# Encoder's end of a two-layer graph network: inverse denominators by transfers, and two node blocks multiplied inside the last attention block

## The chip, the core and the metric

The kernel runs on one core of a Trainium2 chip. The metric is the device time of one execution in microseconds (us). A core has five engines that work side by side, each with its own instruction queue: TensorE (PE in the profile, with PEld for its weight loads), VectorE (DVE), ScalarE (ACT), GpSimd (POOL) and SyncE (SP). Transfers (DMAs) are issued by SP, ACT or POOL and run on 16 shared DMA engines. Matmul results go to PSUM banks of 128 partitions by 512 float32 values, everything else lives in SBUF or in DRAM.

## The reference

Two graph layers on 4096 nodes with 512 features, with one dense 4096 x 4096 mask. The part that matters here is the end of the first layer's encoder and the start of its MLP block (`adj` serves as both patterns, so the two attentions are the same):

```python
Xw = jnp.einsum('hnd,hde->hne', Xh, W)                 # 4 heads of 128 features
sig = jax.nn.sigmoid(f1[:, :, None] + f2[:, None, :])
local_att = _masked_softmax(local_pattern[None] * sig, lmask)
Xa = jnp.einsum('hij,hjd->hid', att, Xw)
Xc = Xa.transpose(1, 0, 2).reshape(n, F)
Xn = _batchnorm(Xc, enc_bn_gamma, enc_bn_beta)         # over the nodes, per feature
emb = _mlp_block(Xn, enc_mlp_W, enc_mlp_b, enc_mlp_bn_gamma, enc_mlp_bn_beta)
# _mlp_block: h = elu(x @ Wm.T + bm) + x, then batchnorm(h)
```

So every output of the attention has to be divided by its softmax denominator, the mean and variance of each feature over all nodes have to be known, and only then can the MLP's product with the normalised features be finished. After it come the decoder (the same attention weights again), its MLP block, and a second graph attention layer, called GAT below.

## The kernel before

All features are kept transposed: a head is a tile of 128 partitions (features) by 4096 nodes, in the tiles R[0] to R[4]. `attention` (L224) runs over 8 *blocks* n, a pair of head and half of the target nodes (2048 each), and in a block over 32 *steps* j of 128 source nodes. In one step ScalarE makes the weight tile e (128 x 2048) with a tanh and an exponential (L571, L572), VectorE multiplies it by the mask (L573), and TensorE multiplies it into four PSUM banks, `po` (L470; the fourth bank joins at step 2, L467). A float32 matmul leaves two records in the profile.

The softmax denominators are sums of e over the steps. Most tiles are summed by VectorE into `acc` (L500, in the last block's last steps L504), some by GpSimd's accumulating transfers into `acc2` (L490), and a few go directly through a matmul with ones (L268). Two last matmul groups with ones turn acc and acc2 into the bank `den`. In blocks 0 to 6 the inverse denominators are made during the next block: a copy of den through DRAM, inverted there in a narrow form (`dcol`, L284 and L285), and sent to all partitions by transfers on GpSimd's queue (L288, L293). Then `scaled` (L686) multiplies each output quarter and `statistics` (L689) takes its mean and variance.

The last block has no next block. Its code begins at L531: the last tile's products (L533, held back so that den comes first), the inverses in one wide form (L546 and L547), the copy of the four outputs out of PSUM (`out_enc`, L683), and for each quarter a matmul with a broadcast column of the identity (L561), which puts the row of inverses on all partitions of a PSUM bank. `scaled` reads that bank. L549 also stores the inverses in DRAM for the decoder.

The MLP block (`mlp_block`, L731) multiplies w (the weights, 4 input blocks by 512 outputs) with the four heads' outputs `xc`. The batchnorm before it is folded in: w is scaled by a_att (`scale_weights`, L696), and its shift becomes part of the bias (`bias_of`, L699, small matmuls with one column each). For heads 0 to 2 this can be done early: `coefs_of_three`, `bias_of_three` and `scale_three` (L710 to L719) are called in the last attention block at steps 10, 12 and 20, through the argument `extras` of L727. After the block, for output block 0, the products of heads 0 to 2 are made for the first 7 of the 8 node blocks (21 matmuls, `product` called at L748), then `last_head` (L776) makes coefficients, bias and weights for head 3, and the 7 sums are completed with its products (L754). There are 7 banks named `ps` (`bank()`) and one named `den` (`bank1()`). The order on each engine is set by a scheduler from the order of the code, with a few explicit ties (`issue_after`, `pinned`).

At the very end of the kernel, GAT's last block already uses another way (L550 to L558): the inverses go to DRAM and come back by four transfers on SyncE's queue into the four parts of acc, and `finish_last` reads these.

Of the kernel before, what the change touches and what calls it, by code (L numbers as in the profile page):

```python
# [39 lines left out]
N, F, H, D, P = 4096, 512, 4, 128, 128  # L40
IB = 512
NIB = N // IB
NJ = N // P
C = IB // P

TB = 2048
NTB = N // TB
SB = TB // IB
# [42 lines left out]
def kernel(ctx, tc, x, xT, adjT, w0, w0T, v0, wencT, wdecT, vecs, w1, w1T, a1, outT):  # L91
    nc = tc.nc
# [10 lines left out]
    w = big.tile([P, C, F], FP, name="w")  # L103

    def nodes(r, ib):
        return r[:, ib * IB:(ib + 1) * IB]
# [4 lines left out]
    def bank():  # L111
        return psum.tile([P, IB], FP, name="ps")
# [12 lines left out]
    ident = consts.tile([P, P], FP, name="ident")  # L125
# [28 lines left out]
    bias = consts.tile([P, C], FP, name="bias")  # L154
# [6 lines left out]
    rinvs = [[dram.tile([1, TB], FP, name=f"rinvs{h}_{t}") for t in range(NTB)] for h in range(H)]  # L161
# [6 lines left out]
    def everywhere(d, row, lo, n):  # L168

        return bass.AP(tensor=d.tensor, offset=d.offset + row * d.shape[-1] + lo, ap=[[0, P], [1, n]])  # L170
# [53 lines left out]
    def attention(what, keep, pools, weights, values, row_of, out, finish, ebufs, modes=None, invert=None,  # L224
                  kept=None, sums=None, sums2=None, extras={}, row0=None, masks0=(), in_parts0=1,
                  finish_last=None, behind=(), fast=None):
# [23 lines left out]
        spool, made, masks0 = pools, 0, list(masks0)  # L250
        if invert is not None:
            acc = spool.tile([P, TB], FP, name="acc") if sums is None else sums
# [143 lines left out]
        for n, (h, tb) in enumerate(blocks):  # L396
            last = n == len(blocks) - 1
# [11 lines left out]
            ahead, late = [], []  # L409
# [121 lines left out]
            for s, b in enumerate(po):  # L531
                for k, t in late:
                    nc.tensor.matmul(b, block(values[h], k), t[:, s * IB:(s + 1) * IB], start=(k == 0),  # L533
                                     stop=(k == NJ - 1))
            if fast is not None:
                combined(h, tb, m)
            outs = [out(spool, h, tb, s, po[s]) for s in range(SB)] if finish_last is None else po
            if invert is None:
                for s, o in enumerate(outs):
                    rb = spread(h, tb, s)  # L540
# [4 lines left out]
            inv = spool.tile([P, IB], FP, name="dsb", tag="rb", bufs=3)  # L545
            nc.vector.tensor_scalar(inv, den, invert[0], None, invert[1])  # L546
            nc.vector.reciprocal(inv, inv)  # L547
            if kept is not None:
                nc.gpsimd.dma_start(rinvs[h][tb].rearrange("o (s i) -> (o s) i", i=IB), inv[0:P:32, :])  # L549
            elif finish_last is not None:  # L550

                nc.sync.dma_start(rinvs[h][tb].rearrange("o (s i) -> (o s) i", i=IB), inv[0:P:32, :])
                rbs = [rb for rb, in in_parts(SB, acc)]
                for s, rb in enumerate(rbs):
                    nc.sync.dma_start(rb, everywhere(rinvs[h][tb], 0, s * IB, IB))
                for s, rb in enumerate(rbs):
                    finish_last(h, tb, s, po[s], rb)
                continue  # L558
            for s, o in enumerate(outs):
                rb = bank()  # L560
                nc.tensor.matmul(rb, ident[:, 32 * s:32 * s + 1].to_broadcast([P, P]), inv, start=True, stop=True)  # L561
                for f in finish:
                    f(spool, h, tb, s, o, rb, True)

    def in_parts(n, *tiles):
        for i in range(n):
            yield tuple(t[:, i * TB // n:(i + 1) * TB // n] for t in tiles)
# [10 lines left out]
    with tc.tile_pool(name="keep", bufs=1) as keep:  # L578

        with tc.tile_pool(name="f_small", bufs=1) as small, tc.tile_pool(name="f_work", bufs=2) as work:  # L580
# [5 lines left out]
            for ib in range(NIB):  # L586
# [7 lines left out]
                for c in range(0, C, 1 if ib == 0 else C):  # L594
                    n = 1 if ib == 0 else C
                    load = nc.sync.dma_start(xs[ib][:, c:c + n, :], xin[:, c:c + n, :])
# [10 lines left out]
            for ib in range(NIB):  # L607
# [15 lines left out]
                for c in range(C):  # L623
                    if ib == 0 and c == 1:
# [3 lines left out]
                    made = (nc.gpsimd if by_pool else nc.vector).tensor_scalar(  # L628
                        hn, xs[ib][:, c, :], mv[:, c, 0:1], rstd[:, c:c + 1], ALU.subtract, ALU.mult)
# [12 lines left out]
                if ib == 0:  # L642

                    pw = bank1()
                    with tc.issue_after(last_pe.ins):
                        for h in range(H):
                            nc.tensor.matmul(pw[:, 2 * h:2 * h + 2], w0Ts[:, h, :], v0s[:, h, :],
                                             start=True, stop=True)
# [4 lines left out]
                for c in range(C):  # L653
                    j = ib * C + c
                    for k in range(2):
                        pv = heads_of(bank())
                        for h in range(2):
                            nc.tensor.matmul(pv[:, h, :], hT[:, 2 * k + h, c * P:(c + 1) * P], w0x[:, 2 * k + h, :],  # L658
                                             start=True, stop=True)
# [19 lines left out]
        xc = [R[4], R[0], R[1], R[2]]  # L679
# [36 lines left out]
        def scale_three(load):  # L716
            nc.vector.tensor_add(bias, banks[0][:, 0:C], vec_of("enc_mlp_b"))
            for fb in range(C - 1):
                scale_weights(fb)  # L719

        with tc.tile_pool(name="enc", bufs=1) as spool:

            with tc.issue_after(last_copy.ins), tc.issue_after(masks0[-1][1].ins):
                attention("enc", keep, spool, tanh_weights, R[0:4], lambda h, tb: (rows[tb], h), out_enc,
                          (scaled, statistics), 6, lambda n: (ENC_FIRST, ENC_SECOND, ENC_THIRD, ENC)[min(n, 3)],
                          (TINY, ALU.max), "write", row0=row0, masks0=masks0,
                          extras={(2, 8): encoder_weights, (H * NTB - 1, 10): coefs_of_three,  # L727
                                  (H * NTB - 1, 12): bias_of_three, (H * NTB - 1, 20): scale_three})


        def mlp_block(work, w, bias, src, dst, gamma, beta, scale, between, early=None):  # L731

            def product(z, o, ib, lo, hi):
                for fb in range(lo, hi):
                    last = nc.tensor.matmul(z, w[:, fb, o * P:(o + 1) * P], nodes(src[fb], ib),  # L739
                                            start=(fb == 0), stop=(fb == C - 1))  # L740
                return last

            for o in range(C):
                zs = {}
                if o == 0:
                    for ib in range(NIB - 1):
                        zs[ib] = bank()
                        product(zs[ib], o, ib, 0, C - 1)  # L748
                    if early is not None:
                        early()  # L750
                for ib in range(NIB):
                    if ib in zs:
                        z = zs[ib]
                        product(z, o, ib, C - 1, C)  # L754
                    else:
                        z = bank()
                        last_product = product(z, o, ib, 0, C)
                    ex = work.tile([P, IB], FP, name="ex")
                    re = work.tile([P, IB], FP, name="re")
                    nc.scalar.activation(ex, z, AF.Exp, bias=bias[:, o:o + 1])  # L760
                    nc.scalar.activation(re, z, AF.Relu, bias=bias[:, o:o + 1])
                    nc.vector.scalar_tensor_tensor(ex, ex, 1.0, re, ALU.min, ALU.add)
                    d = nodes(dst[o], ib)
                    if scale is None:
                        nc.vector.tensor_add(d, nodes(src[o], ib), ex)
                    else:
                        nc.vector.scalar_tensor_tensor(d, nodes(src[o], ib), scale[:, o:o + 1], ex, ALU.mult, ALU.add)
                    made = nc.vector.bn_stats(stats[:, o, ib, :], d)
                    between(o, ib, made)
                bn_coefs(stats, gamma, beta, a_mlp, b_mlp, o, o + 1)  # L770
            return last_product

        with tc.tile_pool(name="m_small", bufs=1) as small, tc.tile_pool(name="m_work", bufs=3) as work:
            yc = [R[3]] + [small.tile([P, N], FP, name=f"yc{o}") for o in range(1, C)]

            def last_head():  # L776
                bn_coefs(stats, "enc_bn_gamma", "enc_bn_beta", a_att, b_att, C - 1, C)
                nc.vector.tensor_add(bias, bias_of(bank1(), C - 1, C)[:, 0:C], bias)
                scale_weights(C - 1)


            behind_it = []
            mlp_block(work, w, bias, xc, yc, "enc_mlp_bn_gamma", "enc_mlp_bn_beta", a_att,
                      lambda o, ib, made: behind_it.append(made) if (o, ib) == (1, 0) else None, last_head)


            for h in range(H):
                w2 = work.tile([P, D], FP, name="w2", bufs=2)
                nc.vector.tensor_scalar_mul(w2, w0Ts[:, h, :], a_mlp[:, h:h + 1])
                bb = work.tile([P, P], FP, name="bb", bufs=1)  # L790
                nc.vector.tensor_scalar_mul(bb, ones, b_mlp[:, h:h + 1])
                pc = bank1()
                nc.tensor.matmul(pc[:, 0:D], bb, w0Ts[:, h, :], start=True, stop=True)
                cr = work.tile([P, 1, D], FP, name="cr", bufs=2)
                nc.vector.tensor_copy(cr[:, 0, :], pc[:, 0:D])
                for ib in range(NIB):
                    pv = bank().rearrange("p (c d) -> p c d", d=D)
                    for c in range(C):
                        nc.tensor.matmul(pv[:, c, :], block(yc[h], ib * C + c), w2, start=True, stop=True)  # L799
                    nc.vector.tensor_add(nodes(xc[h], ib).rearrange("p (c d) -> p c d", d=D), pv,  # L800
                                         cr.to_broadcast([P, C, D]))
# [15 lines left out]
        z = w.rearrange("p c f -> p (c f)")[:, 0:4 * PAIRS * HD].rearrange("p (i k c) -> p i k c", i=4, c=HD)  # L817
# [310 lines left out]
```

## Time and profile before

| what | us |
|---|---|
| median of 3 runs | 3199.43 |
| lowest and highest of them | 3197.14, 3202.03 |
| the profiled execution | 3198.86 |
| its span | 3197.1 |
| transition that the change touches: last record of L470 in the encoder to the first product of head 3 | 1025.22 to 1056.22 |

The profile is one execution; times in its views count from the start of its span. A line of a timeline gives start, length, engine, line of the kernel, operation, output and input with their shape, the number of records, and in square brackets the idle time before and what ended it. A line of the windows gives, for each stretch, the busy time and records of each engine in the order PE, PEld, DVE, ACT, POOL, then the granted TensorE clock, the DMA share and GB/s. Line numbers are those of the kernel before; the changed kernel's lie a few lower in this part.

### The profile page before, as it was taken

The numbers are of one execution on the slowest core, as the hardware profiler recorded it, in microseconds if no ns is written. First come the engines' busy times: TensorE is split into PE (matmuls) and PEld (weight loads), VectorE is DVE, ScalarE is ACT, GpSimd is POOL, SyncE is SP. The second block draws the span as 40 slices with busy tenths as digits, with TensorE's granted clock in tenths as the row PEclk, the third lists the DMA queues.
The fourth block names the chain that finished last, engine by engine and source line by source line (L and its number), as shares of the span: only waits on it lengthen the run. The fifth ranks groups of instructions, "written<-read, shape, count | busy, mean of one in ns | idle before, by whom it ended". The sixth has DMA issues, their size and how long they took to land.

```text
span 3197.1 us, 30054 instructions
## 1 busy us (share of the span) xinstructions
PE 3146.9 (98%) x10539; PEld 1371.7 (43%) x10539; DVE 2938.7 (92%) x2222; ACT 2573.7 (81%) x1825; POOL 525.9 (16%) x680
## 2 busy tenths in 40 slices
PE   7999999999999999999999999999999999999998
PEld 6334444444444463333333333458544444444443
DVE  7989999999999678999999999685699999999998
ACT  7999999999998449999999999466755665666663
POOL 3001211211211000010100100026312222222221
PEclk9999999999999999999999999999999999999999
DMA  9998978988987014444445454322579999899996
GB/s 212 198 194 253 267 209 233 271 223 229 267 227 190 7 44 148 155 159 156 160 162 165 141 168 145 97 105 74 149 193 228 219 219 243 217 213 229 236 213 156
DMA packets 214792, 589.25 MB, mean 184 GB/s; under 512 B 25872, under 2 KB 28976, under 8 KB 198640
## 3 DMA queue, kind: packets, MB, share of 16 engines
q0 software_dynamic: 71008, 231.95, 37.9%
q1 hardware_dynamic: 132200, 332.53, 30.1%
q10 hardware_dynamic: 11432, 22.85, 2.0%
q8 instruction: 83, 1.36, 0.2%
q14 instruction: 69, 0.57, 0.1%
HBM read 378.15 MB, written 84.30 MB: 145 GB/s over the span
## 4 chain that ended last, share of the span: by engine, by line
PE 68%; DVE 15%; issue 8%; ACT 5%; DMA 3%; DVEq 0%; ACTq 0%; POOL 0%; POOLq 0%; SPq 0%
PE ps L470 28%; PE ps L332 22%; PE ps L739 7%; DVE e L573 5%; DVE acc L500 4%; PE den L332 3%; PE ps L950 3%; ACT e L571 3%; DMA a<-mask 3%; DVE R L500 2%; ACT e L572 2%; DVE e L1045 2%; PE den L268 1%; PE ps L799 1%; PE ps L658 1%
## 5 line engine op out<-in xcount | busy, mean ns | idle before, releaser
L470 PE MATMUL ps<-e,R 128*128 128x512 f32 x3992 | 1737.9, 595 | 19.2 <-DVE e L573 16.6
L470 PEld LDWEIGHTS ps<-e,R 128*128 128x128 f32 x3992 | 754.6, 190 | 998.8 <-issue 921.6
L573 DVE TENSOR_TENSOR e<-e,a 128x2048 f32<-128x2048 f32 (+1 forms) x470 | 1049.5, 2261 | 80.2 <-ACT e L572 66.9
L571 ACT ACTIVATE e<-rowb,score 128x2048 f32<-128x2048 f32 (+1 forms) x470 | 909.1, 1969 | 20.3 <-PE ps L332 8.9
L572 ACT ACTIVATE e<-e 128x2048 f32<-128x2048 f32 (+1 forms) x470 | 866.9, 1879 | 4.4 <-DVE e L573 0.7
L332 PE MATMUL ps<-e,R 128*64 128x512 f32 x2624 | 746.8, 592 | 1.6 <-DVE e L573 1.5
L1044 ACT ACTIVATE e<-rowb,nq,jcol 128x2048 f32<-128x2048 f32 x224 | 459.6, 2088 | 263.3 <-DMA w<-e 133.1
L1045 DVE SCALAR_TENSOR_TENSOR e<-e,jcol,a 128x2048 f32<-128x2048 f32 (+1 forms) x265 | 592.9, 2271 | 2.8 <-ACT e L1044 2.8
L332 PEld LDWEIGHTS ps<-e,R 128*64 128x64 f32 x2624 | 241.9, 137 | 319.7 <-issue 316.2
L500 DVE TENSOR_TENSOR R<-R,e 128x2048 f32<-128x2048 f32 x128 | 292.5, 2285 | 0.0
L500 DVE TENSOR_TENSOR acc<-acc,e 128x2048 f32<-128x2048 f32 x122 | 278.7, 2284 | 1.0
L490 POOL DMA_DIRECT2D w<-e x178 | 151.9, 865 | 605.8 <-DMA w<-e 293.1
L739 PE MATMUL ps<-R,w 128*128 128x512 f32 x512 | 220.4, 592 | 0.6 <-DVE w L697 0.6
L490 POOL DMA_DIRECT2D acc<-e x142 | 119.1, 893 | 521.3 <-DMA acc<-e 238.4
L739 PEld LDWEIGHTS ps<-R,w 128*128 128x128 f32 x512 | 97.1, 190 | 123.0 <-issue 117.7
L332 PE MATMUL den<-e,R 128*64 128x512 f32 x320 | 149.8, 592 | 0.0
L332 PE MATMUL ps<-e,w 128*64 128x512 f32 x288 | 138.1, 592 | 0.7 <-DVE e L573 0.7
L293 POOL DMA_DIRECT2D rb<-rinvs x60 | 34.5, 578 | 520.7 <-DVE R L687 449.4
L950 PE MATMUL ps<-w1x,hT 128*128 128x260 f32 x512 | 115.5, 384 | 1.4 <-ACT hT L928 1.4
L332 PE MATMUL ps<-t,w 128*64 128x512 f32 x336 | 111.3, 592 | 1.1 <-DVE t L341 1.1
L950 PEld LDWEIGHTS ps<-w1x,hT 128*128 128x128 f32 x512 | 96.5, 190 | 19.9 <-issue 3.4
L332 PE MATMUL ps<-t,R 128*64 128x512 f32 x192 | 90.2, 592 | 0.0
(209 smaller groups left out, 2115.5 us busy)
## 6 DMA issues: line engine op xcount, KB each, us to landing
a<-mask SPq DMA_DIRECT2D x720, 256.0 KB, 4.3
w<-e POOLq DMA_DIRECT2D x178, 512.0 KB, 6.8
acc<-e POOLq DMA_DIRECT2D x142, 512.0 KB, 7.1
e<-ekeep SPq DMA_DIRECT2D x48, 1024.0 KB, 5.1
ekeep<-e SPq DMA_DIRECT2D x36, 1024.0 KB, 7.1
mask<-in_adjT POOLq DMA_DIRECT2D x8, 2048.0 KB, 105.0
rowb<-rows SPq DMA_DIRECT2D x16, 1024.0 KB, 5.5
rb<-rinvs POOLq DMA_DIRECT2D x60, 256.0 KB, 4.7
```

The source lines that it names most:

```text
L293: hop.dma_start(rb, everywhere(rinvs[h][tb], 0, s * IB, IB))
L332: last_half = nc.tensor.matmul(b[g * HD:(g + 1) * HD, :], weight, x, start=start, stop=stop)
L470: last_main = nc.tensor.matmul(b, block(values[h], j), e[:, s * IB:(s + 1) * IB], start=(j == 0), stop=(j == NJ - 1))
L490: nc.gpsimd.dma_start(into_half, e_half, **({"accum_op": ALU.add} if j > moved[0] else {}))
L500: nc.vector.tensor_add(acc, acc, e)
L571: nc.scalar.activation(e, rowb, AF.Tanh, bias=column(score[:, 1], j, h), scale=0.5)
L572: last_act = nc.scalar.activation(e, e, AF.Exp, scale=0.5)
L573: last_dve = nc.vector.tensor_mul(e, e, a)
L739: last = nc.tensor.matmul(z, w[:, fb, o * P:(o + 1) * P], nodes(src[fb], ib), start=(fb == 0), stop=(fb == C - 1))
L950: m = nc.tensor.matmul(banks[k][:, 0:2 * DX], hT[:, fb, c * P:(c + 1) * P], w1x[:, fb, 2 * k:2 * k + 2, :].rearrange("p h x -> p (h x)"), ...
L1044: last_act = nc.scalar.activation(e, rowb, AF.Relu, bias=column(nq, j, h), scale=column(jcol, j, h))
L1045: last_dve = nc.vector.scalar_tensor_tensor(e, e, column(jcol2, j, h), a, ALU.add, ALU.mult)
```

## The change

Three edits, all at the encoder's end:

1. The four broadcast matmuls of L561 go away. The last block of the encoder now does what GAT's last block does: inverses to DRAM, then four transfers of a row to all partitions, into the four parts of acc. For the encoder they are issued on ScalarE's queue. GAT's end stays as it was.
2. Coefficients, bias and scaled weights of heads 0 to 2 are made at steps 1, 4 and 6 of the last block instead of 10, 12 and 20.
3. The products of heads 0 to 2 for node blocks 0 and 1 (output block 0, 6 matmuls) are made inside the last block, called at steps 9 and 12; `mlp_block` is given their banks and makes the remaining 15.

```diff
-            if kept is not None:
-                nc.gpsimd.dma_start(rinvs[h][tb].rearrange("o (s i) -> (o s) i", i=IB), inv[0:P:32, :])
-            elif finish_last is not None:
-
-                nc.sync.dma_start(rinvs[h][tb].rearrange("o (s i) -> (o s) i", i=IB), inv[0:P:32, :])
-                rbs = [rb for rb, in in_parts(SB, acc)]
-                for s, rb in enumerate(rbs):
-                    nc.sync.dma_start(rb, everywhere(rinvs[h][tb], 0, s * IB, IB))
-                for s, rb in enumerate(rbs):
+            queue = nc.scalar if kept is not None else nc.sync
+            queue.dma_start(rinvs[h][tb].rearrange("o (s i) -> (o s) i", i=IB), inv[0:P:32, :])
+            rbs = [rb for rb, in in_parts(SB, acc)]
+            for s, rb in enumerate(rbs):
+                queue.dma_start(rb, everywhere(rinvs[h][tb], 0, s * IB, IB))
+            for s, rb in enumerate(rbs):
+                if finish_last is not None:
                     finish_last(h, tb, s, po[s], rb)
-                continue
-            for s, o in enumerate(outs):
-                rb = bank()
-                nc.tensor.matmul(rb, ident[:, 32 * s:32 * s + 1].to_broadcast([P, P]), inv, start=True, stop=True)
+                    continue
                 for f in finish:
-                    f(spool, h, tb, s, o, rb, True)
+                    f(spool, h, tb, s, outs[s], rb, True)
...
+        def product(src, w, z, o, ib, lo, hi):
+            for fb in range(lo, hi):
+                last = nc.tensor.matmul(z, w[:, fb, o * P:(o + 1) * P], nodes(src[fb], ib),
+                                        start=(fb == 0), stop=(fb == C - 1))
+            return last
+
+        zs_ahead = {}
+
+        def product_ahead(ib):
+            def f(load):
+                zs_ahead[ib] = bank()
+                product(xc, w, zs_ahead[ib], 0, ib, 0, C - 1)
+            return f
...
-                          extras={(2, 8): encoder_weights, (H * NTB - 1, 10): coefs_of_three,
-                                  (H * NTB - 1, 12): bias_of_three, (H * NTB - 1, 20): scale_three})
+                          extras={(2, 8): encoder_weights, (H * NTB - 1, 1): coefs_of_three,
+                                  (H * NTB - 1, 4): bias_of_three, (H * NTB - 1, 6): scale_three,
+                                  (H * NTB - 1, 9): product_ahead(0), (H * NTB - 1, 12): product_ahead(1)})
...
-        def mlp_block(work, w, bias, src, dst, gamma, beta, scale, between, early=None):
-            def product(z, o, ib, lo, hi):
...
+        def mlp_block(work, w, bias, src, dst, gamma, beta, scale, between, early=None, ahead={}):
             for o in range(C):
                 zs = {}
                 if o == 0:
-                    for ib in range(NIB - 1):
+                    zs.update(ahead)
+                    for ib in range(len(zs), NIB - 1):
                         zs[ib] = bank()
-                        product(zs[ib], o, ib, 0, C - 1)
+                        product(src, w, zs[ib], o, ib, 0, C - 1)
                     if early is not None:
                         early()
```

More of the change, by code (lines that the diff above doesn't have):

```diff
@@ L726 @@
                           (TINY, ALU.max), "write", row0=row0, masks0=masks0,
-                          extras={(2, 8): encoder_weights, (H * NTB - 1, 10): coefs_of_three,
-                                  (H * NTB - 1, 12): bias_of_three, (H * NTB - 1, 20): scale_three})
-        def mlp_block(work, w, bias, src, dst, gamma, beta, scale, between, early=None):
-            def product(z, o, ib, lo, hi):
[L738 to L741, printed above, removed]
+                          extras={(2, 8): encoder_weights, (H * NTB - 1, 1): coefs_of_three,
+                                  (H * NTB - 1, 4): bias_of_three, (H * NTB - 1, 6): scale_three,
+                                  (H * NTB - 1, 9): product_ahead(0), (H * NTB - 1, 12): product_ahead(1)})
+        def mlp_block(work, w, bias, src, dst, gamma, beta, scale, between, early=None, ahead={}):
             for o in range(C):
@@ L753, in mlp_block @@
                         z = zs[ib]
-                        product(z, o, ib, C - 1, C)
+                        product(src, w, z, o, ib, C - 1, C)
                     else:
                         z = bank()
-                        last_product = product(z, o, ib, 0, C)
+                        last_product = product(src, w, z, o, ib, 0, C)
                     ex = work.tile([P, IB], FP, name="ex")
@@ L783 @@
             mlp_block(work, w, bias, xc, yc, "enc_mlp_bn_gamma", "enc_mlp_bn_beta", a_att,
-                      lambda o, ib, made: behind_it.append(made) if (o, ib) == (1, 0) else None, last_head)
+                      lambda o, ib, made: behind_it.append(made) if (o, ib) == (1, 0) else None, last_head,
+                      zs_ahead)
             for h in range(H):
```

## Prediction

> **What bounds the kernel now.** I read the page first: which engine is full, and over how much of the span.
>
> ```profile
> span 3197.1 us, 30054 instructions
> PE 3146.9 (98%) x10539; PEld 1371.7 (43%) x10539; DVE 2938.7 (92%) x2222; ACT 2573.7 (81%) x1825; POOL 525.9 (16%) x680
> ```
>
> TensorE is full for 98% of the span, so a change pays only by taking work off TensorE where it is the late engine, or by filling a hole in it. Then I read the timeline of all engines across the end of the encoder, which is all that the change touches:
>
> ```profile
> 1025.22 1.92 PE L268 MATMUL den<-e,ones 128*32 128x512 f32 x16
> ...
> 1028.79 3.70 PE L533 MATMUL ps<-e,R 128*128 128x512 f32 x8
> 1028.93 0.69 DVE L546 TENSOR_SCALAR dsb<-den 128x512 f32<-128x512 f32 x1 [1.70 <-PE den L268]
> ...
> 1029.66 3.35 DVE L547 RECIPROCAL dsb<-dsb 128x512 f32<-128x512 f32 x1
> ...
> 1033.06 3.70 PE L561 MATMUL ps<-dsb,ident 128*128 128x512 f32 x8 [0.57 <-DVE dsb L547]
> ...
> 1036.60 18.19 PE L739 MATMUL ps<-R,w 128*128 128x512 f32 x42
> ...
> 1054.62 0.95 PE L702 MATMUL den<-coefs,w 128*128 128x1 f32 x8
> ...
> 1056.22 19.15 PE L739 MATMUL ps<-R,w 128*128 128x512 f32 x44 [0.65 <-DVE w L697]
> ```
>
> The reader is to see one TensorE chain without a real hole: denominators, last tile (L533), broadcast of the inverses (L561), 21 products that need only heads 0 to 2 (L739; a matmul leaves two records here, 0.429 us apart), bias, then the products of head 3. Is TensorE also late in the eighth block before it? The timelines of TensorE's weight loads and of VectorE say yes but for one place, step 25:
>
> ```profile
> 1004.42 0.30 PEld L470 LDWEIGHTS ps<-e,R 128*128 128x128 f32 x2 [0.92 <-DVE e L573]
> ```
>
> The usual idle time there is 0.24 us, so TensorE waited 0.68 us for that tile. Last, windows of 1 us gave the granted clock (the number after the brackets):
>
> ```profile
> 958.00:959.00 1.00, 1.00 (x3) 0.42 (x3) 1.00 (x2) 1.00 (x1) 0.12 (x1) 0.96 1.08 238
> 959.00:960.00 1.00, 1.00 (x2) 0.33 (x1) 1.00 (x1) 1.00 (x2) 0.73 (x1) 0.50 0.92 160
> 960.00:961.00 1.00, 1.00 (x2) 0.33 (x1) 1.00 (x2) 1.00 (x1) 0.00 (x0) 0.50 1.13 289
> 961.00:962.00 1.00, 1.00 (x3) 0.44 (x2) 1.00 (x1) 1.00 (x2) 0.00 (x0) 0.50 1.05 274
> 962.00:963.00 1.00, 1.00 (x4) 0.44 (x3) 0.86 (x1) 1.00 (x1) 0.78 (x1) 0.83 1.06 309
> ```
>
> Half rate from about 959.0 to 962.4, just behind the 12 one-column bias matmuls (L702, 955.16 to 957.8): some 1.7 us lost. So there is far less slack in this block than the records' count suggests.
>
> **What the Trainium skill says.** "TensorE: Matmul & The Clock Gate", Part 1, What's actually happening: the array runs at half rate after a low-activity window of about 3.4 us, and the window is free-running. The trace agrees: one dip of 3.4 us at 0.50, behind 2.6 us of one-column work. "DMA: Bandwidth & Descriptors", Two DMAs through the same engine are not ordered: a read of what another transfer wrote must wait for that one's semaphore. Here too: at the kernel's end the write issues at 3182.7 and the first read at 3184.5. Same page, Issuing engines are not separate DMA queues: SyncE's and ScalarE's transfers share the 16 engines, so SyncE's route is a fair price for ScalarE's.
>
> **The change part by part.** T is the end of the denominators (1028.86 before).
>
> *Broadcast off TensorE.* L533's last slot ends at 1028.79 + 8 x 0.429 = 1032.22 and L739 starts at 1036.60: 4.38 us leave TensorE (3.43 of L561, 0.95 of waits around it). -4.38.
>
> *Six products moved into the block.* 6 x 2 x 0.429 = 5.14 us leave the chain behind T. -5.14.
>
> *What they cost inside the block.* As built, three products stand between steps 8 and 9, three before step 12. TensorE works without a hole from 911.8 to step 25: it starts step 2 at 918.78 where VectorE's timeline has the tile by 913.5, step 10 at 948.2 against 940.7. So all 5.14 us push it, less the hole at step 25: +5.14 - 0.68 = +4.46, and T is at about 1033.3.
>
> *Coefficients from step 10 to 1, bias from 12 to 4, scaling from 20 to 6.* No instruction is added. On ScalarE two table loads of 1.28 us and a 0.20 us root (938.44 to 941.25) move ahead of step 4's tile; ScalarE is full either way and is where it was from step 12 on. On VectorE the bias sum (0.12) and the scalings (1.18, 981.49 to 982.67) move from behind to ahead of its idle stretch (1.15, 1.77, 0.97, 0.57 and 0.69 us at L573 from 938 to 963). Tiles 4 to 9 come some 2.5 to 4.5 us later, and TensorE has 6 us in hand at each: cost 0. Tile 25 comes 1.3 us earlier (1003.1), while TensorE arrives at 1008.9, so the hole is gone, and VectorE's last sums are done by about 1026, TensorE needing them at 1031.9. The sum for step 4 makes VectorE wait for the bias matmuls (they end near 928.2, VectorE arrives at 926.8): 1.5 us, soaked up by the same idle stretch. The dcol inversion falls 4 us later, and POOL's rinvs and rb transfers behind it too; their rb is wanted at 965.8, was issued at 945.6, and here near 950 with 4.7 us to land (median of rb on POOL's queue). Cover 10 us; were it late, only VectorE's lead of 5 us would go.
>
> *The new route.* The kernel's own end runs it on SyncE's queue, shown by VectorE's timeline:
>
> ```profile
> 3179.35 3.35 DVE L547 RECIPROCAL dsb<-dsb 128x512 f32<-128x512 f32 x1
> 3187.75 0.75 DVE L1064 SCALAR_TENSOR_TENSOR R<-ps,ssum,R 128x512 f32<-128x512 f32 x1 [5.05 <-DMA R<-rinvs]
> 3188.77 0.75 DVE L1064 SCALAR_TENSOR_TENSOR R<-ps,ssum,R 128x512 f32<-128x512 f32 x1 [0.27 <-DMA R<-rinvs]
> ```
>
> 5.05 us from the inverses to the first product, parts about 1 us apart. At the encoder's end no other transfer runs (0.02 MB from 1026 to 1060), and ScalarE has nothing behind the five issues but the root for head 3 and its table load. After: inverses at T + 4.15 (1033.01 - 1028.86), first scaling at T + 9.20, four scalings and four statistics 4.85 (1035.26 to 1040.11), coefficients 1.6 (1040.14 to 1041.72): T + 15.65. TensorE, with 15 products left, loads the first bias weight at 1054.20 - 1028.86 - 4.38 - 5.14 = T + 15.82. Cover: 0.17 us. Bounds: below nothing is excluded, since the 15 products have to run first whatever lands early; if the parts land 1 us late, 0.8 us of stall; I take 0, as the only measured route gives it. All seven banks are now held at T (four outputs, bias, two ahead); the first product behind L533 gets the bias bank, the next needs L683's first copy at T + 4.8 and is due at T + 5.9: 0.
>
> *POOL* loses one issue (0.59 us), on nobody's path. SyncE's order is unchanged, and so is everything behind the encoder.
>
> Sum: -4.38 - 5.14 + 4.46 = -5.06 us. The profiled execution took 3198.86 (its span 3197.1), giving 3193.8; the median shown is 0.57 higher, so 3194.4.
>
> **The rivals.**
>
> A, *the forecast*: the dip comes again behind the moved bias matmuls, 3194.4.
>
> B, *no dip this time*. Before, a missing dip gains nothing, since TensorE would only wait longer at step 25. After, nothing waits there, so 1.6 us more are saved: -6.7, 3192.7. For it: the window is free-running, and the bias matmuls fill only 2.6 of 3.4 us. Against it: the neighbours are as dense as before.
>
> C, *the cover runs out*. With 0.17 us of cover, a route 2 to 3 us longer stalls TensorE as much, and a longer lull could call up another dip: gain 1 to 3, about 3197.4. For it: the thin cover. Against it: the route measured at the kernel's end.
>
> D, *the transfers replace the broadcast as the bound*, slower. In earlier blocks rinvs took 6.9 us (POOL's queue) and rb 7.4 (ScalarE's): 14.3 instead of 5.05, a stall of 9.1, +4.0 us, with a dip +5.7: 3203.4 to 3205.1. It decides from a route of 10.1 us on. Against it: those ran beside full DMA engines, here they are idle.
>
> That the change doesn't do what it says: the built order shows every move, so I give this nothing.
>
> **How the numbers follow.** A 0.50, B 0.25, C 0.14, D 0.06, 0.05 for what I don't see, half of it slower. 0.2% is 6.4 us, about what a measurement of this kernel can tell from no change; the three runs before spread over 4.9 us. With that scatter A passes 6.4 in three of ten, B in six of ten: faster 0.30. Slower by that much: part of D and of the unseen, 0.07. The rest, 0.63, is within. Range: 3191.3 (B with scatter) to 3198.3 (C).
>
> **What would show it.** T near 1033.3; no L561; step 25 without idle time; the idle time of TensorE between the 15 products and L702 under 0.5 us; head 3's first product at about 1051.2 instead of 1056.2; clock 0.50 near 930 (A) or not (B). Wrong if TensorE waits for a tile between steps 2 and 12, or if the first scaling comes later than 6 us behind the inverses.

## The result and the profile after

The kernel after takes 3192.33 us (median of 11 runs, 3190.36 to 3196.14) against 3199.38 us for the kernel before beside it (11 runs, 3196.71 to 3202.03): a ratio of 0.998, interval 0.9973 to 0.9988. In a second series it took 3192.54 us (17 runs) against 3199.12 us (63 runs), ratio 0.9981 (0.9974 to 0.9988). The means differ by 6.4 and 6.2 us in the two series. The profiled execution of after took 3192.33 us, its span is 3190.4 us.

The page of after, its first lines (span; busy time, share and instructions of each engine):

```profile
span 3190.4 us, 30044 instructions
PE 3139.7 (98%) x10531; PEld 1368.4 (43%) x10531; DVE 2938.4 (92%) x2222; ACT 2573.5 (81%) x1825; POOL 522.3 (16%) x679
```

TensorE's busy time fell by 7.2 us and its instructions by 8: four broadcast matmuls, two records each.

The timeline of TensorE in after, from the last encoder block's start to head 3's products:

```profile
908.15 1.93 PE L268 MATMUL den<-e,ones 128*32 128x512 f32 x16
...
925.56 2.73 PE L697 MATMUL ps<-coefs,w 128*128 128x1 f32 x24
...
947.10 2.74 PE L718 MATMUL ps<-R,w 128*128 128x512 f32 x6
...
962.03 2.74 PE L718 MATMUL ps<-R,w 128*128 128x512 f32 x6
964.60 65.40 PE L470 MATMUL ps<-e,R 128*128 128x512 f32 x152
...
1031.67 1.90 PE L268 MATMUL den<-acc,ones 128*32 128x512 f32 x16
1033.50 3.70 PE L533 MATMUL ps<-e,R 128*128 128x512 f32 x8
1037.04 13.04 PE L718 MATMUL ps<-R,w 128*128 128x512 f32 x30
1049.91 0.95 PE L697 MATMUL den<-coefs,w 128*128 128x1 f32 x8
1051.51 23.87 PE L718 MATMUL ps<-R,w 128*128 128x512 f32 x55 [0.65 <-DVE w L692]
```

The broadcast is gone, L718 follows L533 with nothing between, 15 products instead of 21 (30 records instead of 42) stand behind the block, and two groups of three stand inside it. The bias matmuls run at 925.56 instead of 955.16. Head 3's first product starts at 1051.51 (1056.22 before).

VectorE at the same place, the first scaling and what it waited for; then TensorE's weight load of head 3's bias matmuls:

```profile
1034.44 3.35 DVE L547 RECIPROCAL dsb<-dsb 128x512 f32<-128x512 f32 x1
...
1042.80 0.69 DVE L682 TENSOR_TENSOR R<-R,acc 128x512 f32<-128x512 f32 x1 [2.67 <-DMA acc<-rinvs]
...
1049.37 0.16 DVE L186 TENSOR_TENSOR coefs<-vec,coefs 128x1 f32<-128x1 f32 x1
```

```profile
1049.65 1.12 PEld L697 LDWEIGHTS den<-coefs,w 128*128 128x128 f32 x8 [0.41 <-issue]
```

The scaling now waits for the transfer, as it should; the coefficients come at 1049.53 and the load that needs them follows 0.12 us later, with 0.41 us of idle time instead of the usual 0.24. The cover is used up to the last tenth.

Windows of 2 us of after, of TensorE alone:

```profile
926.00:928.00 2.00, 2.00 (x20) 1.00 0.55 205
928.00:930.00 2.00, 2.00 (x7) 0.81 1.00 199
930.00:932.00 2.00, 2.00 (x4) 0.50 1.15 223
932.00:934.00 2.00, 2.00 (x5) 0.84 0.87 216
```

The half-rate stretch is there again, behind the bias matmuls in their new place: (0.19 + 0.50 + 0.16) x 2 = 1.7 us lost.

To compare executions I use D, the time from the first denominators matmul of encoder block 6 (L268, 908.15 here) to head 3's first product. It takes out whatever ran differently before: in the thirteen profiles of this document D starts between 907.40 and 910.91. D is 147.98 us before and 143.36 after: -4.62. The kernel before starts it here; its end, 1056.22, is in the prediction:

```profile
908.24 1.92 PE L268 MATMUL den<-e,ones 128*32 128x512 f32 x16
```

Nothing is lost or won again until the last block of GAT: the first matmuls behind the encoder's MLP (L799 at 1148.39 before, L800 at 1143.67 after) and VectorE's last tile (it ends at 3173.81 before, 3169.07 after) are both 4.7 us earlier. From head 3's first product to that tile, twelve of the thirteen profiles have 2117.56 to 2117.60 us; the exception, e4, is explained below.

Of the other 2 us of the 6.7 between the spans, 1.8 arise at the kernel's very end, the last block of GAT, which the change doesn't touch. TensorE there, before and then after:

```profile
3169.40 1.06 PE L268 MATMUL den<-e,ones 128*32 128x512 f32 x8 [2.33 <-DVE e L1045]
3170.40 1.76 PE L533 MATMUL ps<-e,R 128*128 128x512 f32 x2
3173.87 1.94 PE L268 MATMUL den<-e,ones 128*32 128x512 f32 x8 [1.71 <-DVE e L1045]
3175.57 1.94 PE L268 MATMUL den<-w,ones 128*32 128x512 f32 x8
3177.28 1.19 PE L268 MATMUL den<-R,ones 128*32 128x512 f32 x8
```

```profile
3164.65 1.67 PE L268 MATMUL den<-e,ones 128*32 128x512 f32 x8 [2.32 <-DVE e L1046]
...
3169.12 1.06 PE L268 MATMUL den<-e,ones 128*32 128x512 f32 x8 [0.79 <-DVE e L1046]
3170.00 1.04 PE L268 MATMUL den<-w,ones 128*32 128x512 f32 x8
3170.86 1.04 PE L268 MATMUL den<-R,ones 128*32 128x512 f32 x8
```

The same eight records take 1.94 us in one and 1.04 in the other. TensorE waits for VectorE's tiles here, and in both executions the granted clock falls to 0.50: before, from 3170.8 to 3177.6, under the last three groups, so that the denominators end 4.66 us behind VectorE's last tile; after, from 3165.0 to 3168.4, where the wait for the next tile takes it in, and they end 2.83 us behind it. That is which part of the end the stretch meets in one execution, and says nothing of the change: e6 below, whose encoder is that of the kernel before but for the order of its bias matmuls, ends as after does, and e7, a form of the changed kernel, has a late end (4.3 us).

### The profile page after: what moved, and what is told of

It reads as the page before. It is cut to its first block, busy times and chain, and to the rows that moved or that the text cites. A ratio compares the mean times of both kernels' runs of the same rounds, so it can differ in the third digit from the quotient of the medians.

```text
span 3190.4 us, 30044 instructions
## 1 busy us (share of the span) xinstructions
PE 3139.7 (98%) x10531; PEld 1368.4 (43%) x10531; DVE 2938.4 (92%) x2222; ACT 2573.5 (81%) x1825; POOL 522.3 (16%) x679
## 4 chain that ended last, share of the span: by engine, by line
PE 54%; DVE 21%; issue 12%; ACT 8%; DMA 4%; DVEq 0%; POOL 0%; ACTq 0%; POOLq 0%; SPq 0%
PE ps L332 22%; PE ps L470 14%; PE ps L718 7%; DVE e L1046 6%; DVE R L500 6%; ACT e L566 5%; DVE e L568 4%; PE den L332 3%; PE ps L951 3%; DVE acc L500 3%; ACT e L567 3%; DMA a<-mask 3%; PE den L268 1%; PE ps L800 1%; DMA acc<-e 1%
## 5 line engine op out<-in xcount | busy, mean ns | idle before, releaser
L718 PE MATMUL ps<-R,w 128*128 128x512 f32 x512 | 220.8, 592 | 0.6 <-DVE w L692 0.6
L718 PEld LDWEIGHTS ps<-R,w 128*128 128x128 f32 x512 | 97.1, 190 | 123.0 <-issue 116.7
```

## The experiments

Two theories stood at the start. The first: taking the broadcast off TensorE brings the 4.4 us, and the products moved ahead add only what they fill of the hole at step 25. The rival: the moves bring it, and the route costs more than it saves. Later the question became why the medians differ by more than D. All results first; the ratio is against the kernel before in the same series, and "half rate" is what each one's profile shows between steps 1 and 16 of the last encoder block.

| kernel | median us (runs) | ratio, interval | D us | half rate |
|---|---|---|---|---|
| before | 3199.38 (11) | | 147.98 | yes |
| after | 3192.33 (11) | 0.998 (0.9973 to 0.9988) | 143.36 | yes |
| e1, route alone | 3193.79 (21) | 0.9987 (0.9981 to 0.9994) | 143.73 | no |
| e2, moves alone | 3197.25 (13) | 0.9996 (0.9988 to 1.0004) | 147.69 | yes |
| e3, one block ahead | 3191.54 (14) | 0.9979 (0.9971 to 0.9987) | 141.67 | no |
| e4, three blocks ahead | 3196.56 (13) | 0.9995 (0.9987 to 1.0004) | 144.09 | no |
| a2, after again | 3192.54 (17) | 0.9981 (0.9974 to 0.9988) | 141.67 | no |
| e5, after, bias split | 3192.00 (21) | 0.9981 (0.9975 to 0.9988) | 141.72 | no |
| e7, one ahead, bias split | 3192.28 (19) | 0.9981 (0.9974 to 0.9988) | 141.67 | no |
| e8, as e7, busy end | 3191.40 (17) | 0.9978 (0.9971 to 0.9986) | 141.67 | no |
| e6, before, bias split | 3197.25 (13) | 1.0000 (0.9992 to 1.0008) | 147.98 | no |
| e9, after, busy end | 3192.25 (19) | 0.9983 (0.9976 to 0.9989) | 143.59 | yes |
| e10, before, busy end | 3197.67 (13) | 0.9999 (0.9990 to 1.0007) | 147.99 | yes |

The kernel before took 3198.06 us beside e1 to e4, 3199.12 beside a2 to e8 and 3197.45 beside e6, e9 and e10.

**e1, the route alone.** Coefficients, bias and scaling back at steps 10, 12 and 20, no product ahead, and the 21 products tied behind the last tile, so that none of them can be scheduled into the block:

```diff
-                          extras={(2, 8): encoder_weights, (H * NTB - 1, 1): coefs_of_three,
-                                  (H * NTB - 1, 4): bias_of_three, (H * NTB - 1, 6): scale_three,
-                                  (H * NTB - 1, 9): product_ahead(0), (H * NTB - 1, 12): product_ahead(1)})
+                          extras={(2, 8): encoder_weights, (H * NTB - 1, 10): coefs_of_three,
+                                  (H * NTB - 1, 12): bias_of_three, (H * NTB - 1, 20): scale_three})
...
-                        product(src, w, zs[ib], o, ib, 0, C - 1)
+                        with pinned(tail):
+                            product(src, w, zs[ib], o, ib, 0, C - 1)
```

> Route alone: coefficients, bias and scaling stay at steps 10, 12 and 20, no product is made ahead, all 21 are tied behind the last tile; only the broadcast goes by transfers. D is the time from the first denominator matmul of block 6 to head 3's first product: 147.98 us before, 143.36 after. Theory (the route carries nearly all of the gain, 4.38 us, because the 21 products hide it): D 143.6, time about 3195. Rival (the moved products carry it, and the route alone saves only the 0.95 us of waits): D 147, time about 3198.5.

D is 143.73, 4.25 us under the kernel before, as the first theory has it. The coefficients come at 1044.16, and the weight load that waits for them is due at 1049.10, so 4.9 us of cover stand where after has none. The timeline shows both ends of D, and between them what the moves would still have to give:

```profile
907.40 1.92 PE L270 MATMUL den<-e,ones 128*32 128x512 f32 x16
...
1003.60 20.87 PE L472 MATMUL ps<-e,R 128*128 128x512 f32 x48 [1.80 <-DVE e L570]
...
1051.13 24.30 PE L720 MATMUL ps<-R,w 128*128 128x512 f32 x56 [0.65 <-DVE w L694]
```

The hole at step 25 is open, and wider than in the kernel before, which had a half-rate stretch ahead of it.

**e2, the moves alone.** After, with the broadcast by matmul in place of the route:

```diff
-            queue = nc.scalar if kept is not None else nc.sync
-            queue.dma_start(rinvs[h][tb].rearrange("o (s i) -> (o s) i", i=IB), inv[0:P:32, :])
...
+            for s, o in enumerate(outs):
+                rb = bank()
+                nc.tensor.matmul(rb, ident[:, 32 * s:32 * s + 1].to_broadcast([P, P]), inv, start=True, stop=True)
```

> Moves alone: coefficients at 1, bias at 4, scaling at 6, two node blocks ahead, but the broadcast is again the four matmuls of before. Theory (TensorE is late in the block too, so moving fills only the hole at step 25): D 147.3 with a half-rate window behind the bias, 145.7 without one, time about 3198.5 or 3197. Rival (the moved products carry the gain): D 143.5, time about 3194.5.

D is 147.69, with the half-rate stretch at 930 to 935: the moves alone are worth 0.3 us in such an execution. The rival falls. The median is 0.8 us under the kernel before, an interval that includes no change.

**e3 and e4, one and three node blocks ahead.** e3 drops the product at step 12 (and ties the other 18 behind the last tile), e4 adds one at step 15:

```diff
-                                  (H * NTB - 1, 9): product_ahead(0), (H * NTB - 1, 12): product_ahead(1)})
+                                  (H * NTB - 1, 9): product_ahead(0), (H * NTB - 1, 12): product_ahead(1),
+                                  (H * NTB - 1, 15): product_ahead(2)})
```

> The changed kernel with one node block ahead instead of two, the other 18 products tied behind the last tile. Theory (a moved product costs TensorE the same inside the block; one block of 2.57 us already fills the hole): D 143.4, the same as after, and the cover of the transfers is 2.6 us longer, so TensorE doesn't wait for head 3's coefficients. Rival (each moved block pays 2.57 us): D 145.9.

> The changed kernel with a third node block ahead, at step 15, so that 12 products are left to hide the transfers. Theory (the cover is used up at two, so the denominators come 2.57 us later and nothing is given back): D 145.9, with TensorE idle 2.6 us before the bias matmuls of head 3, time about 2.6 us above after. Rival 1 (there is slack in the block): D 143.4. Rival 2 (each moved block pays): D 140.8.

e3's D is 141.67 without a half-rate stretch:

```profile
908.41 1.92 PE L270 MATMUL den<-e,ones 128*32 128x512 f32 x16
...
1050.08 25.16 PE L720 MATMUL ps<-R,w 128*128 128x512 f32 x58 [0.65 <-DVE w L694]
```

The kernel after without a stretch (a2 below) has 141.67 as well, so the second node block ahead buys nothing; it only takes the cover, 2.5 us here (counted to the weight load; the expectation of e7 counts 2.9 to the matmul behind it), down to none. In e4 the limit shows. TensorE's timeline, then the windows behind it:

```profile
1039.20 10.57 PE L718 MATMUL ps<-R,w 128*128 128x512 f32 x24 [1.19 <-DVE R L678]
...
1050.49 1.02 PE L697 MATMUL den<-coefs,w 128*128 128x1 f32 x8 [0.72 <-DVE coefs L186]
```

```profile
1050.00:1052.00 2.00, 1.02 (x8) 1.00 0.00 0
1052.00:1054.00 2.00, 1.84 (x4) 0.82 0.00 0
1054.00:1056.00 2.00, 2.00 (x4) 0.50 0.00 0
1056.00:1058.00 2.00, 2.00 (x5) 0.83 0.00 0
```

With 12 products left behind the block TensorE waits for a bank and then for the coefficients. The third block costs its 2.57 us inside and saves almost nothing behind (17.79 us from the denominators to head 3's first product, 17.94 in after): D is 2.42 us above e3's. The longer lull is followed by a half-rate stretch of its own, and VectorE's last tile of GAT comes 1.7 us later for it, 2119.27 us behind head 3's first product. Together that is 4.1 of the 4.5 us by which e4's mean gain (1.7) falls short of e3's (6.2) in the same series.

**a2, the kernel after once more**, and **e5**, with its bias matmuls spread out:

```diff
+        def bias_part(o):
+            def f(load):
...
+                for fb in range(C - 1):
+                    nc.tensor.matmul(banks[0][:, o:o + 1], w[:, fb, o * P:(o + 1) * P], b_att[:, fb:fb + 1],
+                                     start=(fb == 0), stop=(fb == C - 2))
...
-                                  (H * NTB - 1, 4): bias_of_three, (H * NTB - 1, 6): scale_three,
+                                  **{(H * NTB - 1, 3 + o): bias_part(o) for o in range(C)}, (H * NTB - 1, 8): scale_three,
```

> The kernel after once more, unedited. D is the stretch from the first denominators matmul of encoder block 6 to head 3's first product behind the last block: 143.36 us in its first profile, with the half-rate clock stretch behind the bias matmuls of step 4 in it. Theory (the half-rate stretch falls or doesn't fall by chance, and there is no slack left in the last block to soak it up): D is either 143.4 with it or 141.7 without it, and nothing between. Rival (the stretch follows the bias matmuls every time): D 143.4 again, half rate near 930.

> The kernel after, with the twelve one-column bias matmuls in four parts of three at steps 3 to 6 and the weights scaled at step 8. Theory (a lull of 2.6 us of one-column matmuls is what lets the clock fall; four lulls of 0.65 us are too short for it): no half-rate stretch in the last block, D 143.36 - 1.65 = 141.7, and the median at or below the kernel after's of the same call, by 0 to 1.7 us, by how often the kernel after has the stretch. Rival (the stretch has another cause than the lull): half rate again between 925 and 940, D 143.4.

The same program, another execution. TensorE's timeline and windows in a2:

```profile
908.00 1.92 PE L268 MATMUL den<-e,ones 128*32 128x512 f32 x16
...
925.41 2.73 PE L697 MATMUL ps<-coefs,w 128*128 128x1 f32 x24
...
1048.07 0.95 PE L697 MATMUL den<-coefs,w 128*128 128x1 f32 x8
1049.67 12.71 PE L718 MATMUL ps<-R,w 128*128 128x512 f32 x29 [0.65 <-DVE w L692]
```

```profile
928.00:930.00 2.00, 2.00 (x7) 1.00 1.02 201
930.00:932.00 2.00, 2.00 (x6) 1.00 1.06 209
```

Full rate throughout, and D = 1049.67 - 908.00 = 141.67, which is 1.69 us less. So the program alone doesn't decide whether the stretch comes, and in after it is paid in full. Among the profiles with the undivided lull it is in before, after, e2, e9 and e10, and not in e1, e3, e4 and a2; among the four with the lull in parts (e5, e6, e7, e8) in none. Five of nine against none of four points to the lull, without settling it. The median of e5 is 0.5 us under a2's, which these runs can't tell from nothing.

**e6, the same split in the kernel before.**

```diff
-                                  (H * NTB - 1, 12): bias_of_three, (H * NTB - 1, 20): scale_three})
+                                  **{(H * NTB - 1, 12 + o): bias_part(o) for o in range(C)}, (H * NTB - 1, 20): scale_three})
```

> The kernel before, with its twelve bias matmuls in four parts of three at steps 12 to 15, one step's products between them. Theory (the kernel before has slack in its last block: TensorE reaches tile 25 before VectorE has made it, so that half rate ahead of it is taken out of the wait): no half rate, the wait at step 25 grows from 0.68 to about 2.3 us, D stays 147.98, the time that of the kernel before within 0.5 us. Rival (half rate costs the kernel before its 1.65 us as well): the wait stays 0.68, D 146.3, the time 1.6 us less where the stretch would have fallen.

D is 147.98 again, to the hundredth, without a half-rate stretch, and the time that of before. TensorE's weight loads at step 25 of e6, to be held against the line shown in the prediction (0.92 us of idle time there):

```profile
1001.54 0.19 PEld L470 LDWEIGHTS ps<-e,R 128*128 128x128 f32 x1 [0.24 <-issue]
1004.34 0.30 PEld L470 LDWEIGHTS ps<-e,R 128*128 128x128 f32 x2 [2.61 <-DVE e L573]
1004.88 0.19 PEld L470 LDWEIGHTS ps<-e,R 128*128 128x128 f32 x1 [0.24 <-issue]
```

What the clock doesn't take, the wait takes: tile 25 sets the time in the kernel before. On this point the two kernels differ: after has no wait there that could take the stretch in.

**e7, e8, e9, e10: a busy end.** e7 is e3 with the bias matmuls split; e8 is e7, e9 after and e10 before, each with two matmuls whose product nobody reads ahead of each of the last two terms of the denominators in GAT's last block (the expectations say decoder; the edit acts only where `finish_last` is set, and that is GAT's):

```diff
                     if held and j + 1 not in by_ones:
-                        with tc.issue_after(last_main.ins):
-                            for t in held:
+                        for t in held:
+                            if finish_last is not None and last and j == NJ - 1:
+                                last_main = stay_busy(last_main, 2)
+                            with tc.issue_after(last_main.ins):
                                 add_to_den(den, t, not begun)
...
```

> One node block multiplied ahead instead of two, and the bias matmuls in four parts. Theory (the second node block ahead buys nothing, since the coefficients of head 3 then come no earlier than TensorE needs them, and the split keeps the clock up): head 3's bias matmuls wait for nothing, cover 2.9 us, no half rate in the last block, D 141.7 as in the one-ahead run; median about 3198.2 - 7 = 3191. Rival (one block ahead leaves 0.86 x 3 us more behind the last block): D 141.7 + 2.57 = 144.2.

> The kernel of one block ahead and split bias, and in the decoder's last attention block two idle matmuls of 512 columns ahead of each of the last two denominators' terms, where TensorE otherwise waits 2.3 us for VectorE's weights. Their product is not used. Theory (the last 1.8 us of the difference between the two kernels came from a half-rate stretch that these waits bring about at the kernel's end, earlier or later by chance): no half rate behind 3160, the denominators end 2.9 us behind VectorE's last addition, and the slow end of the run-to-run spread goes; median 0 to 1.8 us under the same kernel without them. Rival (that stretch is no matter of these waits): half rate near the end as often as before, the same median, or slower by the 0.86 us of the product that now comes behind.

> The kernel after, with the two pairs of unused 512-column matmuls at the decoder's end only. Theory (half rate at the kernel's end, brought about by TensorE's two waits there, costs up to 1.9 us in some runs): no half rate behind 3160, the denominators end 2.9 us behind VectorE's last addition, the median 0.5 to 1.5 us under the kernel after's, some 3191.4. Rival (no matter of these waits): half rate there as before, median as the kernel after's, 0.9981 of before.

> The kernel before, with the two pairs of unused 512-column matmuls at the decoder's end only; its encoder is not touched. Theory (the half rate at the end has nothing to do with the change, and the kernel before pays for it as well): no half rate behind 3160, the denominators end 2.9 us behind VectorE's last addition instead of 4.74, median 0.5 to 1.8 us under the kernel before. In its encoder D is 148.0 whether or not the half-rate stretch falls there: with it the wait at step 25 is 0.7, without it 2.3. Rival: no difference from the kernel before, and D 146.3 without the half-rate stretch.

e7 confirms e3: D 141.67, and head 3's bias matmuls wait for nothing. With the busy end no profile shows half rate between 3160 and 3180 (none of three), and the denominators end 2.8 us behind VectorE's last tile; without it six of ten profiles do, though only before and e7 with a cost at the end. But the medians did not move: 0.9983 for e9 against 0.9981 for a2, 0.9999 for e10, and e8 0.9 us under e7, within the intervals. VectorE's last product in e10 shows a price:

```profile
3191.31 0.75 DVE L1068 SCALAR_TENSOR_TENSOR R<-ps,ssum,R 128x512 f32<-128x512 f32 x1 [0.47 <-PE ps L537]
```

The idle matmuls displace a real product that had run in the wait (32 records of it stand behind the denominators now, 30 before), and the last output waits for TensorE, 0.47 us in e10, 0.40 in e9 and 0.29 in e8. Whether that price alone keeps the median where it was isn't shown. The highest times are lower (3199.18 in e10, 3200.62 for the kernel before beside it; 3194.97 in e9, 3195.89 and 3196.14 in after), but e10's 13 runs stand against 39; the theory's gain in the median did not come. e8 has the lowest median of all, but none of e3, e7 and e8 can be told from the kernel after.

## Why the prediction was right, and where it was off

The forecast's direction and mechanism held: the route alone brings 4.25 us, as e1 shows with the moves taken away, and the moves bring what they fill of the hole. The time forecast, 3194.4, came out 2 us too high; rival B's 3192.7 is nearer. That the measured median lies in the forecast's range is partly luck: the range had room for A and for B, and no step of the forecast had GAT's end, which moved by 1.8 us between the two profiles. By its steps:

- *Broadcast off TensorE, -4.38.* e1 measured -4.25. Right.
- *Six products behind T, -5.14.* From T to head 3's first product the profile has 17.94 us instead of 27.36, -9.42 for both steps together; -9.52 was forecast. Right.
- *Their cost inside, +5.14 - 0.68.* This is the term that was mis-sized. T moved by 4.80 us (1033.57 - 908.15 against 1028.86 - 908.24), not 4.46. The hole of 0.68 us was read off the weight loads' idle time, but behind a wait two loads go out together in 0.30 us: before, the load ahead of the wait starts at 1003.32 and the third one behind it at 1004.96, 1.64 us for three pitches of 0.429 = 1.29. TensorE lost 0.35 us there, not 0.68.
- *The hole has two sizes.* 0.35 us holds only where the half-rate stretch had already delayed TensorE. Without it the hole is 2.05 us (e6: 1004.88 - 1001.54 - 1.29), and filling it is worth as much: e1's D less e3's is 2.06. The sums close: T comes 5.14 - 0.35 = 4.79 us later in after (4.80 measured), 5.14 - 2.05 = 3.09 in a2 (3.11). So the gain is 4.62 us in an execution of after with the stretch, 6.31 without (147.98 - 141.67), and in the kernel before the stretch makes no difference. Rival B described exactly this, and e6 and e10 show its premise; A had only the size of its own, smaller hole wrong. Which of the two is the usual execution the runs don't tell: the mean differences of 6.4 and 6.2 us lie at B's end (6.31), but the interval of the second series, 0.9974 to 0.9988, is 3.8 to 8.3 us and holds both, and e9 against e10, which have the busy end alike, differ by 5.7 us in the mean, between the two.
- *Moving coefficients, bias and scaling, 0.* Right. VectorE waits 2.24 us for the bias matmuls (1.5 forecast), and 8.01 us for the denominators at the block's end all the same, so there was room for it.
- *The route, 5.05 us, cover 0.17, stall 0.* The route took 5.01 us (1042.80 - 1037.79). The cover was nil: the first load waited 0.17 us more than usual, and the products behind it start 2.45 us behind the last load before it, as in e3, which doesn't wait (2.46). Right in this execution; e9, below, shows how thin the cover is, and e4 how near rival C was: one more node block ahead and nearly the whole block's 2.57 us are lost. Rival D, the slower case, had no part in it: in all nine profiles with the route on ScalarE's queue it took 5.0 to 5.4 us.
- *Signs.* T at 1033.57 (1033.3), no L561, no wait at step 25, head 3's first product at 1051.51 (1051.2), half rate near 930: all as listed for A in this execution.

The encoder of e9 is that of after, and there the cover didn't hold: the route took 5.39 us, the bias matmuls start 0.16 us later than the 30 records ahead of them allow (12.87 us at 0.429 each), and head 3's first product comes 18.17 us behind T in place of 17.94, a stall of 0.23 us:

```profile
1036.92 13.04 PE L722 MATMUL ps<-R,w 128*128 128x512 f32 x30
1049.95 1.02 PE L701 MATMUL den<-coefs,w 128*128 128x1 f32 x8
1051.62 10.57 PE L722 MATMUL ps<-R,w 128*128 128x512 f32 x24 [0.65 <-DVE w L696]
```

What stays open: with the stretch in some executions of after, the mean gain from D alone should lie between 4.6 and 6.3 us, and two of the three profiles of this encoder (after, a2, e9) have it. How often it falls in unprofiled runs wasn't measured, nor how often the end's half rate takes its 1.8 us from either kernel, so the means of 6.2 and 6.4 can't be split between the two.

## What to carry to other kernels

A wait that follows a disturbance is slack for it: measure a hole in an execution with the disturbance and in one without, since filling it turns a loss that was free into one that is paid. Work moved from behind a chain into a block where the same engine is late pays only for the hole that it fills (2.06 us of the first node block). Up to the cover of the chain more of it is neutral (the second node block: D 141.67 with it and without), and past the cover each matmul moved costs nearly its full time (the third: 2.4 us lost for 2.6 moved). Size a hole by the start times on both sides of it, not by the idle time that stands beside one load.

## What the hardware showed that was not expected

The clock's half-rate stretch followed a stretch in which TensorE is shown as fully busy: 24 records of one-column matmuls in 2.6 us, 100% in the windows, then 3.4 us at 0.50 or none at all, in the same program (after and a2). The Trainium skill, "TensorE: Matmul & The Clock Gate", Part 1, What's actually happening, puts half rate behind an idle window of about 3.4 us and has that window free-running. The length of the stretch agrees, which is as far as the prediction's "the trace agrees" holds, and its coming in one execution and not in the next fits a free-running window. No profile here shows an idle window ahead of it: that one-column work may count as idle is only suggested, by five of nine profiles with the lull in one piece and none of four with it in parts. A stretch of 3.4 us at half rate takes 1.7 us from TensorE; D grows by as much (143.36 against 141.67) where no later wait takes it in.

A weight load that waited is followed by the next one at once. In the kernel before, these stand on both sides of the line that the prediction shows:

```profile
1003.32 0.19 PEld L470 LDWEIGHTS ps<-e,R 128*128 128x128 f32 x1 [0.24 <-issue]
...
1004.96 0.19 PEld L470 LDWEIGHTS ps<-e,R 128*128 128x128 f32 x1 [0.24 <-issue]
```

Between them two loads take 0.30 us, in before, e6 and e1 alike, so that TensorE made good 0.33 us of the wait in before (0.68 of idle time, 0.35 lost) and 0.32 in e6 (2.37 and 2.05).
